# Layer 3's last sums in another order, leftover tests in front of them, and one wide product folded into a small one

## The chip, the cores and the metric

The kernel runs on one core of one Trainium2 chip. The metric is device time in microseconds, the median of a few executions. A core has TensorE (PE, matrix products into PSUM), VectorE (DVE), ScalarE (ACT), GpSimd (POOL) and SyncE (SP), each with an instruction queue of its own that it works through in order; the queues wait for one another by semaphores.

## The reference, cut to what matters

The model is four graph layers over 4096 nodes with 64 features. Each layer normalizes x, applies relu, passes the result through a layer with the 4096 x 4096 adjacency matrix of zeros and ones, and adds that to x. The change lies in the last one, layer 3, from the sums over the adjacency on:

```python
def weighted_midpoint_lincomb(A, X):
    gamma = lambda_x(X)
    num = A @ (gamma * X)
    den = A @ (gamma - 1.0)
    sgn = jnp.where(den >= 0.0, 1.0, -1.0)
    den = sgn * jnp.maximum(jnp.abs(den), DEN_EPS)
    two_mean = num / den
    mid = mobius_scalar_mul(0.5, two_mean)
    alpha = jnp.sum(A, axis=1, keepdims=True)
    return mobius_scalar_mul(alpha, mid)
...
XW = mobius_matvec(W, X)
AXW = weighted_midpoint_lincomb(A_hat, XW)
return expmap0(jax.nn.relu(logmap0(AXW)))
```

`mobius_scalar_mul`, `logmap0` and `expmap0` scale each row by a function (tanh, artanh) of its length. So per node the layer needs 64 sums of `num`, one of `den`, one of `alpha`, and then a chain of small row-wise operations.

## The kernel before, in words

The adjacency is kept on the chip as 0/1 tiles in fp8 (`A8`), made by a load that casts. That casting load is only right if the matrix holds nothing but zeros and ones, and so `checks()` loads each such tile once more in fp32 (`whole`) and has VectorE test it (1024 wide, with an accumulated count in `odd`). Every 16 tests, and at the end, the counts are summed into `odds`; at the very end PE adds `odds` over the partitions by a one-column product (`flag_ps`), VectorE casts that to `flag`, and all engines read the flag to choose between this kernel and a general one. The tests are background work.

An object `Weave` decides, while the program is built, in which order the instructions of the foreground (the sums on PE) and of the pieces of other work stand in each engine's queue. It keeps an estimated time per engine. `weave.add` puts in a generator of operations; `weave.draw()`, called between products, puts in those operations that would be ready by then; `weave.until(key, DONE)` forces pieces until a result is marked done; background pieces (`weave.back`) are left alone while `weave.quiet` is true. It is set true at the last chunk of layer 2. Once built, the order is fixed: each engine runs its queue in that order, whatever the real times.

Nodes are 32 blocks of 128 (`NB`), in four quarters of 8 blocks (`QB`, `NQ` is 4). Layer 3's features of quarter q, `S3[q, 0]` and `S3[q, 1]`, come from the end of layer 2 by `post2b` and `pre3`, one quarter after another; the key `(4, q)` is marked when quarter q is there. Each row of S3 has 196 numbers: three bf16 parts of the 65 features, and a one for `alpha`.

The outputs are eight chunks u of 512 nodes. `sum3(u, place, lo, hi)` adds blocks lo to hi into chunk u: for each of four groups of 128 nodes, one product per block, with a 128 x 128 piece of A as weights and S3 as the moving part, 196 wide. A chunk's sums lie in two one-bank PSUM tiles (place 0 and 1) or in one two-bank tile (place 2). A full chunk is 128 products, a quarter 32. `take3(u)` folds them out of PSUM: ScalarE copies the first 65 columns and alpha, VectorE adds the other two parts, and, if the chunk was summed in two goes, the part of before (`n65`, `alpha`). `summed` collects chunks: a group of three (or one chunk alone) becomes one generator `post3`, which does the row-wise chain: sign, squares of the row and of its relu, their sums `ss`, a reciprocal square root by steps (`guess`, `nt`, `ny`), artanh by Ln and by a polynomial (`po`), tanh, then x + the result, and the store. In `post3`, `r` is the tile `ny`: its first half belongs to the row's length, its second, `r[:, nb:]`, to the relu's. A predicated copy chooses between the two forms of artanh. Ln and tanh need different ScalarE tables, which `preload` brings in.

`layer3` before: chunks 0, 1, 2 sum quarters 0 and 1 and are folded as "early" parts. Then chunks 3, 4, 5 go through the quarters 0 to 3 side by side: all three quarter 0, all three quarter 1, and so on, each quarter when it is done. After that `quiet` ends and what is left of the tests is put into VectorE's queue. Then chunks 0, 1, 2 take quarters 2 and 3, and last the chunks 6 and 7 take all blocks, each as a group alone.

Of the kernel before, what the change touches and what calls it, by code (L numbers as in the profile page):

```python
# [13 lines left out]
ALU = mybir.AluOpType  # L14
# [555 lines left out]
NQ = 4  # L570
QB = 8
# [33 lines left out]
class Weave:  # L605
# [52 lines left out]
    def free(self, ps):  # L658
        k = ps.tensor.name
        self.banks[self.kind.pop(k)].append(self.used[k][0])  # L660
# [131 lines left out]
def fast_kernel(ctx: ExitStack, tc: tile.TileContext, t: dict, out: bass.AP, flag: bass.AP):  # L792
# [13 lines left out]
    NB = N // P  # L806
# [10 lines left out]
    weave = Weave()  # L817
    free = weave.free

    def one(name):  # L820
        return weave.take(1, lambda: psp.tile([P, CW], F32, tag="one", name=name, bufs=4))

    def two(name):
        return weave.take(2, lambda: psp.tile([P, 2 * CW], F32, tag="two", name=name, bufs=2))
# [4 lines left out]
    def b2(name, shape=(P, QB, D), dtype=F32):  # L829
        return b2p.tile(list(shape), dtype, tag="b2", name=name)  # L830

    def stat(name, n):
        return small.tile([P, ST], F32, tag="st", name=name)[:, :n]
# [3 lines left out]
    DV, AC, GP, SY = (Engine(weave, x.e, x.real, True) for x in (V, S_, G_, Y_))  # L837
# [79 lines left out]
    def rows(s, width=D):  # L917
        return s[:, :, None].to_broadcast([P, s.shape[1], width])
# [12 lines left out]
    def recip(v):  # L931
        r = stat("rc", v.shape[1])
        yield DV.reciprocal(r, v)
        return r
# [38 lines left out]
    def mm(o, lhsT, rhs, start=True, stop=True):  # L973
        weave.wait(names(lhsT, rhs), names(o))
        book_pe(o, lhsT, rhs, 4 if lhsT.dtype == F32 else 1)
        nc.tensor.matmul(o, lhsT, rhs, start=start, stop=stop, skip_group_check=True)  # L976
# [52 lines left out]
    DONE = set()  # L1029
# [545 lines left out]
    def lengths(s):  # L1575

        yield DV.tensor_scalar(s, s, NORM_EPS2, None, op0=ALU.max)
        r = yield from rsqrt(s)
        n = stat("norm", s.shape[1])
        yield DV.tensor_tensor(n, s, r, ALU.mult)  # L1580
        return n, r
# [5 lines left out]
    def preload(func):  # L1587

        yield AC.activation(void, tab, func)
# [80 lines left out]
    def sum3(u, place, lo, hi):  # L1670

        if u not in dst:
            v = [two("acc3")] if place > 1 else [one("acc3") for _ in range(2)]
            dst[u] = lo, [x.rearrange("p (k n) -> p k n", n=256) for x in v]
        start, v = dst[u]
        for d in range(CB):
            o = v[0][:, d, :W3] if len(v) == 1 else v[d // 2][:, d % 2, :W3]
            cols = slice((u % 2) * CW + d * P, (u % 2) * CW + (d + 1) * P)
            for b in range(lo, hi):

                mm(o, A8[u // 2][b // 2][:, b % 2, cols], S3[b // QB, b % QB // CB][:, b % CB, :],
                   start=b == start and d % 2 == 0, stop=b == hi - 1)
                if b % 4 == 3:
                    weave.draw()

    def layer3():

        half = NB // 2
        sets = (0, 1, 2), (3, 4, 5)
        early = {}  # L1690
        for k in range(2):
            for place, u in enumerate(sets[0]):
                weave.until((4, k), DONE)
                sum3(u, place, k * QB, k * QB + QB)
                if k:
                    early[u] = take3(u)
        for lo, hi in ((0, 1), (1, 2), (2, 3), (3, 4)):
            for place, u in enumerate(sets[1]):
                weave.until((4, lo), DONE)
                sum3(u, place, lo * QB, hi * QB)  # L1700
                if hi == NQ:
                    summed(u, take3(u))
        weave.quiet = False
        while weave.back and weave.back[0][1].e == "D":
            weave.issue(weave.back[0])
        for place, u in enumerate(sets[0]):
            sum3(u, place, half, NB)
            summed(u, take3(u, early.pop(u)))
        for place, u in enumerate((6, 7)):
            sum3(u, place, 0, NB)  # L1710
            summed(u, take3(u), alone=True)
        while weave.back:
            weave.force(True)
        others = nc.values_load(flag)
        weave.finish()
        return others
# [3 lines left out]
    def summed(u, parts3, alone=False):  # L1720
        group.append((u, parts3))
        if alone or len(group) == 3:
            weave.add(post3(group[:]))
            group.clear()
# [3 lines left out]
    def take3(u, more=None):  # L1728

        e = D + 1  # L1730
        n65 = b2("n65", (P, CB, e))
        alpha = stat("alpha", CB)
        at = 0
        for ps in dst.pop(u)[1]:
            k = ps.shape[1]
            o = n65[:, at:at + k, :]
            S_.activation(o, ps[:, :, :e], AF.Copy)
            S_.activation(alpha[:, at:at + k], ps[:, :, 3 * e], AF.Copy)
            V.tensor_tensor(o, o, ps[:, :, e:2 * e], ALU.add)
            V.tensor_tensor(o, o, ps[:, :, 2 * e:3 * e], ALU.add)  # L1740
            at += k
            free(ps)
        if more is not None:
            V.tensor_tensor(n65, n65, more[0], ALU.add)
            V.tensor_tensor(alpha, alpha, more[1], ALU.add)
        return n65, alpha

    def post3(parts3):

        nb = CB * len(parts3)
        sgn, den, ss = stat("sgn", nb), stat("den", nb), stat("ss", 2 * nb)
        part = [slice(i * CB, (i + 1) * CB) for i in range(len(parts3))]
        vs = [n65[:, :, :D] for u, (n65, al) in parts3]
        for h, v, (u, (n65, al)) in zip(part, vs, parts3):
            d = n65[:, :, D]
            yield DV.tensor_scalar(sgn[:, h], d, 0.0, 2.0, op0=ALU.is_ge, op1=ALU.mult)  # L1760
            yield DV.scalar_tensor_tensor(v, rows(sgn[:, h]), -1.0, v, op0=ALU.add, op1=ALU.mult)
            sq = b2("sq")
            yield AC.activation(sq[:, :CB, :], v, AF.Square)
            yield DV.scalar_tensor_tensor(sq[:, CB:, :], v, 0.0, v, op0=ALU.max, op1=ALU.mult)
            yield DV.tensor_scalar(den[:, h], d, -1.0, DEN_EPS, op0=ALU.mult, op1=ALU.max)
            yield DV.tensor_tensor(den[:, h], den[:, h], d, ALU.max)
            yield DV.tensor_reduce(ss.rearrange("p (k b) -> p k b", k=2)[:, :, h],
                                   sq.rearrange("p (k b) d -> p k b d", k=2), AX.X, ALU.add)
        yield from preload(AF.Ln)
        rd = yield from recip(den)  # L1770
        n, r = yield from lengths(ss)
        t = stat("t", nb)
        yield DV.tensor_tensor(t, n[:, :nb], rd, ALU.mult)
        ratio = stat("ratio", nb)

        def between():
            yield DV.tensor_tensor(ratio, n[:, nb:], r[:, :nb], ALU.mult)
            for h, v in zip(part, vs):
                yield DV.scalar_tensor_tensor(v, v, 0.0, rows(r[:, nb:][:, h]), op0=ALU.max, op1=ALU.mult)

        a = yield from artanh2(t, between())
        for h, (u, (n65, al)) in zip(part, parts3):
            yield DV.scalar_tensor_tensor(a[:, h], a[:, h], 0.25, al, op0=ALU.mult, op1=ALU.mult)
        yield DV.scalar_tensor_tensor(a, a, ARTANH_MAX, ratio, op0=ALU.min, op1=ALU.mult)
        yield AC.activation(a, a, AF.Tanh)
        for h, v, (u, (n65, al)) in zip(part, vs, parts3):
            yield DV.tensor_tensor(v, v, rows(a[:, h]), ALU.mult)
            x = X[u // 2][:, (u % 2) * CB:(u % 2 + 1) * CB, :]
            yield DV.tensor_tensor(x, x, v, ALU.add)
            yield SY.dma_start(out_nm[:, u * CB:(u + 1) * CB, :], x)  # L1790
# [13 lines left out]
    for step in range(2):  # L1804
        weave.add(load_gates(step))
        layer2(step, post2b if step else post2a)
    others = layer3()
    return others

# [84 lines left out]
```

## Time and profile before

| | |
|---|---|
| time, median of 3 | 811.44 us (811.31 to 813.11) |
| span of the profiled execution | 810.7 us |
| busy in the span: PE, DVE, ACT, POOL | 95%, 79%, 49%, 8% |
| PE's clock granted, mean | 0.988 |
| last op of VectorE that forms quarter 3 of S3 | starts 737.3, two of 0.84 us in all |
| ScalarE's first copies of chunk 5, chunk 7 (last bank) | 751.34, 789.64 |
| last add of VectorE | starts 805.05 |
| last store | issued 805.51 |

The trace names an operation by the engine, the line (nearly all stand in one helper's line, L781, so the tile names tell them apart), the output and inputs, and their size. `n` is `n65`, `acc` the PSUM sums, `whole` a tile under test. What matters here is not an engine's share of the whole span but which engine's queue the last operations stand in, and what the first of them waited for. Each line of the chain of waits is a start, a length and the engine and tile that the end depended on at that time.

### The profile page before, as it was taken

What the parts mean: (1) busy time and instruction counts of PE and PEld (TensorE: products, weight loads), DVE (VectorE), ACT (ScalarE), POOL (GpSimd) and SP (SyncE); (2) the same over time, 40 slices, a digit from 0 to 9 for tenths busy, and PEclk for the clock granted to TensorE, in tenths of its full rate; (3) what the DMA queues carried; (4) which work ended last, traced back from release to release, by engine and by line L of the source; (5) the groups of instructions that cost most, each with busy time, mean ns of one, the idle gap of its engine ahead of it and who ended that gap; (6) DMA issues with size and microseconds to landing.
All of it is one profiled execution on the core that took longest, in us unless ns stands there. A gap on an engine that the chain in (4) does not pass through costs nothing.

```text
span 810.7 us, 12099 instructions
## 1 busy us (share of the span) xinstructions
PE 772.4 (95%) x4473; PEld 355.6 (44%) x4494; DVE 638.3 (79%) x1433; ACT 396.9 (49%) x613; POOL 60.9 (8%) x125
## 2 busy tenths in 40 slices
PE   5999999999999999999999999999999999999990
PEld 2334444444433323333333333444444354699990
DVE  6886777677678788888888888878788787774896
ACT  5655555565565657567666664022220244462333
POOL 3333233230000000000000000000000000000000
PEclk9999999999999999999999999999999999999995
DMA  9999999998301032022022007696888910000010
GB/s 221 151 178 168 202 160 190 197 160 188 108 14 40 0 113 71 0 73 84 0 66 78 13 1 255 240 323 234 293 289 317 326 38 1 2 2 2 1 37 21
DMA packets 43954, 98.39 MB, mean 121 GB/s; under 512 B 5104, under 2 KB 20464, under 8 KB 43888
## 3 DMA queue, kind: packets, MB, share of 16 engines
q1 hardware_dynamic: 25888, 78.98, 29.0%
q0 software_dynamic: 15840, 14.42, 19.0%
q10 hardware_dynamic: 2160, 4.14, 1.4%
q8 instruction: 37, 0.61, 0.3%
q14 instruction: 29, 0.24, 0.1%
HBM read 135.54 MB, written 5.24 MB: 174 GB/s over the span
## 4 chain that ended last, share of the span: by engine, by line
PE 85%; DVE 10%; issue 1%; ACT 1%; DMA 1%; SPq 0%; ACTq 0%; DVEq 0%
PE acc L976 51%; PE score L976 14%; PE cnt L976 13%; DVE n L781 2%; PE rz L976 2%; DVE sig L781 2%; PE ps_t L980 1%; PE ps_l L976 1%; DVE ss L781 1%; DMA whole<-in_adjT 1%; DVE nt L781 1%; PE ps_kq L976 1%; PE ih L976 1%; ACT sig L781 1%; PE ps_n L980 1%
## 5 line engine op out<-in xcount | busy, mean ns | idle before, releaser
L781 ACT ACTIVATE sig<-score,fatt_add,fatt_mul 128x1024 f32<-128x1024 f32 x128 | 148.1, 1200 | 86.9 <-PE score L976 86.3
L781 DVE TENSOR_TENSOR sig<-sig,A 128x1024 f32<-128x1024 f32 x128 | 151.5, 1221 | 40.2 <-ACT sig L781 39.5
L781 DVE SCALAR_TENSOR_TENSOR whole<-whole 128x1024 f32<-128x1024 f32 x128 | 153.1, 1219 | 6.0 <-DMA whole<-in_adjT 5.6
L781 ACT ACTIVATE w<-cnt 128x512 int16<-128x512 f32 x198 | 111.2, 595 | 89.8 <-PE cnt L976 88.5
L976 PE MATMUL score<-qd,kT 64*128 64x512 f32 x512 | 129.6, 623 | 0.0
L976 PE MATMUL acc<-sig,S 128*64 128x512 f32 x512 | 125.7, 608 | 1.5 <-DVE sig L781 1.4
L976 PE MATMUL acc<-A,hm 128*128 128x512 fp8e4 x512 | 115.7, 380 | 0.0
L976 PEld LDWEIGHTS <-hm 128*128 128x128 bf16 x768 | 73.4, 98 | 90.1 <-issue 10.0
L976 PE MATMUL cnt<-A,ftri 128*128 128x512 fp8e4 x256 | 97.7, 384 | 8.2 <-ACT A L781 8.0
L976 PE MATMUL cnt<-A,fupd 128*128 128x512 fp8e4 x248 | 95.5, 385 | 2.6 <-DVE w L781 1.5
L976 PE MATMUL acc<-S,A 128*128 128x196 bf16 x1024 | 88.2, 247 | 0.0
L976 PEld LDWEIGHTS <-A 128*128 128x128 fp8e4 x1024 | 87.1, 96 | 1.1 <-issue 0.8
L976 PEld LDWEIGHTS score<-qd,kT 64*128 64x128 f32 x512 | 44.0, 187 | 81.2 <-ACT sig L781 39.2
L781 DVE TENSOR_SCALAR w<-cnt 128x512 int16<-128x512 f32 x58 | 40.1, 691 | 45.4 <-PE cnt L976 41.0
L976 PE MATMUL acc<-w,hm 128*128 128x512 bf16 x235 | 71.0, 379 | 0.9 <-issue 0.2
L860 POOL DMA_DIRECT2D A<-in_adjT x110 | 59.2, 540 | 120.0 <-DMA A<-in_adjT 119.1
L976 PEld LDWEIGHTS acc<-sig,S 128*64 128x64 f32 x512 | 30.5, 136 | 83.5 <-issue 39.9
L976 PEld LDWEIGHTS <-lo 128*64 128x64 bf16 x768 | 36.8, 109 | 58.4 <-issue 36.2
L976 PE MATMUL acc<-A,lo 128*64 128x512 fp8e4 x512 | 59.2, 381 | 0.0
L781 ACT ACTIVATE mt<-acc 64x512 f32<-64x512 f32 x32 | 18.9, 591 | 67.6 <-PE acc L976 67.1
L976 PEld LDWEIGHTS <-fupd 128*128 128x128 bf16 x248 | 24.3, 98 | 46.1 <-issue 24.3
L1655 POOL MEMSET S<- 128x4 bf16 x8 | 0.9, 116 | 546.9 <-PE ps_l L976 502.2
(185 smaller groups left out, 640.1 us busy)
## 6 DMA issues: line engine op xcount, KB each, us to landing
whole<-in_adjT SPq DMA_DIRECT2D x128, 512.0 KB, 7.1
A<-in_adjT POOLq DMA_DIRECT2D x110, 128.0 KB, 13.6
qd<-qs SPq DMA_DIRECT2D x16, 128.0 KB, 2.8
mx<-gs SPq DMA_DIRECT2D x16, 128.0 KB, 8.1
xT<-gs SPq DMA_DIRECT2D x8, 256.0 KB, 7.3
x<-in_x SPq DMA_DIRECT2D x6, 256.0 KB, 6.5
xs<-x SPq DMA_DIRECT2D x4, 256.0 KB, 4.8
qs<-qT ACTq DMA_DIRECT2D x4, 256.0 KB, 6.4
```

Of the source, the lines that this page charges most:

```text
L781: return fn(*args, **kw)
L860: nc.gpsimd.dma_start(A8[q][b // 2][:, b % 2, :], a)
L976: nc.tensor.matmul(o, lhsT, rhs, start=start, stop=stop, skip_group_check=True)
L980: nc.tensor.transpose(o, src, ident)
L1655: nc.gpsimd.memset(S3[q, c][:, :, 3 * e:], 1.0)
```

## The change

Three edits.

1. The order of the last sums. Chunks 3, 4, 5 sum quarters 0 and 1 as before. Then chunks 3 and 4 alone sum quarter 2. After the wait for quarter 3 come chunk 3's quarter 3, chunk 4's quarter 3, and chunk 5's quarters 2 and 3 together. Each chunk is folded when its sums end. The aim is that chunks 3 and 4 are ready sooner after the wait.
2. The leftover tests. The end of `quiet` and the loop that issues them stand right behind the wait for quarter 3, in front of these sums and of the folds, where they stood behind them.
3. The closing product. Before, `between` multiplied each chunk's relu by the reciprocal length (256 wide per chunk), and after tanh the chunk was multiplied by the factor `a`. Now the factor itself (4 columns per chunk) is multiplied by the reciprocal length, and the relu goes into the last wide operation.

```diff
-        for lo, hi in ((0, 1), (1, 2), (2, 3), (3, 4)):
+        for k in range(2):
             for place, u in enumerate(sets[1]):
-                weave.until((4, lo), DONE)
-                sum3(u, place, lo * QB, hi * QB)
-                if hi == NQ:
-                    summed(u, take3(u))
+                sum3(u, place, k * QB, k * QB + QB)
+        for place, u in enumerate(sets[1][:2]):
+            weave.until((4, 2), DONE)
+            sum3(u, place, half, half + QB)
+
+        weave.until((4, NQ - 1), DONE)
         weave.quiet = False
         while weave.back and weave.back[0][1].e == "D":
             weave.issue(weave.back[0])
+        for place, u in enumerate(sets[1]):
+            sum3(u, place, half + QB if place < 2 else half, NB)
+            summed(u, take3(u))
         for place, u in enumerate(sets[0]):
             sum3(u, place, half, NB)
             summed(u, take3(u, early.pop(u)))
...
         def between():
             yield DV.tensor_tensor(ratio, n[:, nb:], r[:, :nb], ALU.mult)
-            for h, v in zip(part, vs):
-                yield DV.scalar_tensor_tensor(v, v, 0.0, rows(r[:, nb:][:, h]), op0=ALU.max, op1=ALU.mult)
...
         yield AC.activation(a, a, AF.Tanh)
+        yield DV.tensor_tensor(a, a, r[:, nb:], ALU.mult)
         for h, v, (u, (n65, al)) in zip(part, vs, parts3):
-            yield DV.tensor_tensor(v, v, rows(a[:, h]), ALU.mult)
+            yield DV.scalar_tensor_tensor(v, v, 0.0, rows(a[:, h]), op0=ALU.max, op1=ALU.mult)
```

## The prediction

> **What bounds the kernel now.** I read the page's shares first, then busy time by stretch, then the chain of waits, then VectorE in order of time. The page gives PE 95% and DVE 79%, but that is a mean over stages; the change lies in the last 75 us. There the stretches say this (per engine: busy us and instructions, then granted clock, DMA share, GB/s):
>
> ```profile
> core 0: us, PE busy (x) PEld busy (x) DVE busy (x) ACT busy (x) POOL busy (x), PEclk, DMA share, GB/s
> 719.00:738.20 19.20, 19.20 (x228) 19.20 (x227) 16.39 (x79) 10.50 (x24) 0.23 (x2) 1.00 0.01 1
> 738.20:751.30 13.10, 13.10 (x157) 13.10 (x155) 2.33 (x8) 1.37 (x8) 0.00 (x0) 1.00 0.01 3
> 751.30:767.80 16.50, 16.50 (x197) 16.30 (x195) 14.87 (x60) 5.72 (x18) 0.00 (x0) 1.00 0.00 1
> ...
> 789.60:805.50 15.90, 0.01 (x1) 0.00 (x0) 13.61 (x72) 7.41 (x15) 0.00 (x0) 0.64 0.06 19
> ```
>
> PE never pauses from 719.0 to 789.6. VectorE idles from 738.2 to 751.3 (2.33 of 13.10 us busy), then is full, and for 16 us after PE has stopped it alone works. The chain of waits (start, us, what) shows where it passes from PE to VectorE:
>
> ```profile
> 743.99 7.32 PE acc L976 x86
> 751.31 0.02 issue
> 751.34 0.39 ACT n L781
> ...
> 751.82 0.44 DVE n L781
> ...
> 752.71 2.30 DVE whole L781 x4
> 755.01 0.02 issue
> 755.03 0.18 DVE odd L781
> 755.21 0.02 issue
> 755.23 0.16 DVE odds L781
> ```
>
> So up to 751.3 the end is set by PE's sums of chunk 5, after that by VectorE's queue. Its first entry is two leftover tests of adjacency tiles, which are nothing to do with chunk 5. Their data were issued at 642.5 us and such loads land in a median 7.1 us, so they could have run any time after about 650. The last lines of VectorE (start, us, form, idle before) are the closing arithmetic of chunk 7:
>
> ```profile
> 803.37 0.15 DVE L781 TENSOR_TENSOR ratio<-norm,ny 128x4 f32<-128x4 f32 x1
> 803.44 0.42 DVE L781 SCALAR_TENSOR_TENSOR n<-n,ny 128x256 f32<-128x256 f32 x1
> 803.77 0.16 DVE L781 COPY_PREDICATED rc<-flow,po 128x4 f32<-128x4 int32 x1
> ...
> 804.60 0.42 DVE L781 TENSOR_TENSOR n<-n,rc 128x256 f32<-128x256 f32 x1 [0.27 <-ACT rc L781]
> 805.05 0.43 DVE L781 TENSOR_TENSOR X<-X,n 128x256 f32<-128x256 f32 x1
> ```
>
> [...] What an op costs in a queue is its spacing, which I take from the trace: a dependent small op starts 0.20 us after the one before it, a dependent 256-wide one 0.46, an independent one after a 256-wide one 0.34, after a small one 0.07 to 0.09. [...]
>
> **The change part by part.**
>
> PE's order. The built order shows that chunk 5's third quarter (32 products) goes from in front of the wait for S3_3 to just behind chunk 4; nothing else of PE moves but the test's one-column product. From 751.34 to 789.64 (ScalarE's first reads of chunk 5's and chunk 7's last bank) PE did 448 products and that one (0.12 us): 38.18/448 = 0.0852 us each. So chunk 3's last quarter starts 32 x 0.0852 = 2.7 us sooner, at about 740.4 instead of 743.15. It needs S3_3, whose last VectorE op ends at 737.74 + 0.42 = 738.16: 2.2 us of room, no stall. Chunks 3 and 4 end 2.7 us sooner, chunk 5 does not. What do the first two win? Nothing at once: their arithmetic enters VectorE's queue only when `summed` has all three, behind chunk 5's folding.
>
> The tests. They cost 2.69 us on VectorE (752.62 to 755.31). They now stand ahead of the folds of chunk 3, from 738.16 to about 740.9, when VectorE is idle. Behind them in PE's queue stands the one-column product, 20 products into chunk 3's last quarter, so at 742.1: 1.2 us after the tests end, no stall, 0.12 us of PE ahead of chunk 5's end. Chunk 3's folds wait for that product's cast, then for sums that are ready at 742.2: nothing late waits there. Group (3,4,5) begins at 751.94 + 0.80 = 752.74 instead of 755.31: 2.57 won.
>
> The closing product. `between` loses a 256-wide product per chunk, 0.34 us of queue each. Added after tanh, in the path, is one 128x12 (or 128x4) product, 0.20. The last product takes the relu in and stays 0.42 wide. Per group of three: 1.02 off, 0.20 on. For chunk 7 the saving is smaller: without the wide product the predicated copy would start at 803.49 instead of 803.77, and tanh could start at 804.08, just after its table at 804.06, instead of 804.36; then 0.20 goes on: 0.08 won.
>
> I then walked VectorE's new order with the spacings of before, and with PE's ends as the earliest times of the folds (0.48 us from PE's end to the first fold):
> - Group (3,4,5): squares and sums 3 x 1.88 from 752.74 = 758.38; chunk 0's first fold 0.53; reciprocal to `ny` 1.94 (762.39 to 764.33) = 760.85; second fold with the early part 0.94; `norm` to the ratio of artanh 1.18 = 762.97; chunk 1's first fold 0.53; polynomial 1.29; predicated copy to the min 0.63 = 765.42; chunk 1's second fold 0.94; new product 0.20; two chunks' closing 1.60 = 768.16. Chunk 2's sums end at 751.34 + 0.12 + 192 x 0.0852 = 767.82, so its fold starts at 768.30 (0.14 waited), takes 1.39; last chunk's closing 0.80; chunk 0's sign 0.46. Its first squares start at 770.95; before 774.15. **3.20 won.**
> - Group (0,1,2): squares 4.95 = 775.90; to the polynomial 3.60 less one fold plus two folds = 780.04; polynomial 1.26; to the min 0.64 and a sign 0.07 = 782.0; tanh back at 782.30; product 0.20; closing with chunk 6's sign 2.74. Chunk 6's squares start at 785.24; before 789.36. **4.12 won.**
> - Chunk 6: `ss` at 785.86; to `at` 3.13 = 788.99; chunk 7's first fold and two small ops to 789.89. There VectorE meets chunk 7's second fold, whose sums come with PE's end: 790.02 as before. From here PE's end counts again and some of the 4.12 is lost. Fold and flag load to 790.99 (as before); polynomial, tanh, closing and chunk 7's sign 3.27; chunk 7's `ss` at 794.88, before 798.61.
> - Chunk 7: 4.68 to the end of the polynomial, then 0.20, 0.39, 0.20 to tanh, 0.24 back, 0.20 and 0.46: last add at 801.25, before 805.05. **3.80 won**; 811.44 - 3.80 = **807.6 us**.
>
> **The rivals.**
> Partial: ScalarE's queue, in which the copies of the folds stand behind Square, table loads and tanh, holds a fold at two or three places; each such miss costs a table load, 1.28 us. For it: before, chunk 6's second copy ran at 779.95, after a load, though its sums were there at 778.7. Against it: by my walk each copy is ready 0.3 us or more ahead, the last folds of chunks 2 and 7 apart. One miss: 811.44 - 3.80 + 1.28 = 808.9; with a half miss more, 809.4.
> More: VectorE reaches chunk 7 early and its chain starts at PE's end. From the fold's end 790.65, sign, product, squares and sums 1.1, then 6.87 from `ss` to the end: 798.7, 6.8 won, 804.7. Against it: chunk 6's closing stands in front in the order.
> Slower: chunk 5's third quarter was PE's filling while S3_3 was formed. If PE now waits there, 32 products (2.72 us) come late, all sums with them, and if the end is then PE's: 811.44 + 2.7 = 814.1. For it: S3_3 and the test are now waited for with 2.2 and 1.2 us of room instead of 5. Against it: everything up to S3_3 stands in the same order, so 738.2 should hold.
>
> **How the numbers follow.** The walk 0.77, the partial 0.12, more 0.04, slower 0.07. Unknown are each spacing's rounding (over 100 steps, about 0.5 us), the waits of ScalarE, and the run-to-run spread of before, 811.31 to 813.11. The range takes in the walk with 1.4 us below it, since DVE steps that I took as dependent may not be, and the partial case above: 806.2 to 809.4. Faster by over 0.3% means under 809.0: the walk, more, and a part of the partial case, 0.84; within it 0.10, slower 0.06.
>
> **What would show it.** In VectorE's order of time: the tests at 738 to 741; no idle but 0.1 us at chunk 2's fold and at chunk 7's; the group of three starting at 752.7; last add at about 801.2. In PE's: no gap at 740 to 743, end at 789.6. The waits list should show no entry of PE on VectorE. Wrong would be a PE gap there, or ScalarE's copies delaying folds by a table load.

## The result and the profile after

The changed kernel takes 809.23 us (median of 7, 807.69 to 809.48) against 811.52 us for the kernel before (median of 7 in the same comparison, 811.31 to 813.11). The ratio is 0.9962, with a 95% interval of 0.9952 to 0.9972: 3.1 us less (2.3 to 3.9), by the ratio. The forecast was 807.6 us in a range of 806.2 to 809.4, and "faster by over 0.3%".

The executions of each kernel gather around two times some 1.5 us apart. In the traces of before and after PE's granted clock is 0.50 for 3.4 us near 291 us, in code that the kernels share; e1's trace has no such fall there, and its S3 is formed 737.32 - 735.87 = 1.45 us sooner than that of before (last section). The median of before fell to the lower group (811.3) and that of after to the upper (809.2). So I compare traces by a difference that is free of this: from the start of the last op pair that forms S3 (`S<-s3v`, "S3 formed" below) to the start of VectorE's last add (`X<-X,n`). It is 805.05 - 737.32 = **67.73 us** before and 801.48 - 737.23 = **64.25 us** after, so 3.48 us won.

Busy time by stretch, after the change, for the stretch behind the forming of S3 and for the one behind PE's end (same columns as in the prediction):

```profile
738.20:751.30 13.10, 13.10 (x156) 12.90 (x155) 4.87 (x15) 1.37 (x8) 0.00 (x0) 1.00 0.01 3
...
789.60:801.50 11.90, 0.00 (x0) 0.00 (x0) 9.95 (x55) 5.98 (x13) 0.00 (x0) 0.63 0.04 12
```

PE's row is as full as before. VectorE's busy time in the first stretch went from 2.33 to 4.87 us: the tests have moved into it. From 789.6 to the start of the last add PE is done and the chain is VectorE's, 11.9 us where it was 15.4; with the last add it has 55 instructions there instead of 72. VectorE in order of time (start, us, form, idle before) shows the move:

```profile
737.98 1.22 DVE L781 SCALAR_TENSOR_TENSOR whole<-whole 128x1024 f32<-128x1024 f32 x1
...
739.13 1.22 DVE L781 SCALAR_TENSOR_TENSOR whole<-whole 128x1024 f32<-128x1024 f32 x1
...
740.59 0.16 DVE L781 TENSOR_TENSOR odds<-odds,odd 128x1 f32<-128x1 f32 x1
742.18 0.15 DVE L781 CAST flag<-flag_ps 1x1 int32<-1x1 f32 x1 [1.42 <-PE flag_ps L976]
```

The tests end at 740.75, then VectorE waits 1.42 us for the one-column product. That wait costs nothing that counts: the first fold behind it starts at 742.25, some 0.2 us after ScalarE's copies of its sums (741.72 to 742.06), and it is chunk 5's fold at 751.95, behind 4.93 us of idle time, that matters. The chain of waits after the change passes there from PE to VectorE and straight on into the group of three:

```profile
742.02 0.12 PE flag_ps L976 x2
742.14 9.30 PE acc L976 x108
...
751.46 0.39 ACT n L781
...
751.95 0.44 DVE n L781
...
752.83 0.09 DVE sgn L781
```

Where `whole` and `odds` stood (752.71 to 755.39), there is now the group's arithmetic. The list of VectorE's waits from 738 us on (what waited, for what: us in total, times, longest) has four entries:

```profile
DVE n L781 <- ACT alpha L781: 7.3, 4, 4.9
DVE flag L781 <- PE flag_ps L976: 1.4, 1, 1.4
DVE rc L781 <- ACT rc L781: 0.5, 2, 0.3
DVE flow L781 <- issue: 0.4, 1, 0.4
```

The first two lie before 751.95. After that VectorE waits three times in 49.5 us: for tanh at 782.53 (0.20) and at 800.82 (0.27), and 0.36 for the reading of the flag into the engines' registers at 791.09. The last lines are:

```profile
801.02 0.42 DVE L781 SCALAR_TENSOR_TENSOR n<-n,rc 128x256 f32<-128x256 f32 x1
801.48 0.42 DVE L781 TENSOR_TENSOR X<-X,n 128x256 f32<-128x256 f32 x1
```

### The profile page after: what moved, and what is told of

It is laid out like the page before. It is cut to its first block, busy times and chain, and to the rows that moved or that the text cites. A ratio compares the mean times of both kernels' runs of the same rounds, so it can differ in the third digit from the quotient of the medians.

```text
span 807.3 us, 12119 instructions
## 1 busy us (share of the span) xinstructions
PE 774.2 (96%) x4494; PEld 356.5 (44%) x4494; DVE 637.3 (79%) x1429; ACT 397.4 (49%) x613; POOL 60.6 (8%) x125
## 4 chain that ended last, share of the span: by engine, by line
PE 86%; DVE 9%; ACT 1%; issue 1%; DMA 1%; SPq 0%; ACTq 0%; DVEq 0%
PE acc L976 51%; PE score L976 14%; PE cnt L976 14%; PE rz L976 2%; DVE n L781 2%; DVE sig L781 2%; PE ps_t L980 2%; PE ps_l L976 1%; DVE ss L781 1%; DMA whole<-in_adjT 1%; DVE nt L781 1%; PE ps_kq L976 1%; PE ih L976 1%; ACT sig L781 1%; DVE rc L781 1%
## 5 line engine op out<-in xcount | busy, mean ns | idle before, releaser
L976 PE MATMUL acc<-w,hm 128*128 128x512 bf16 x256 | 75.8, 379 | 0.0
```

## The experiments

All in one table; "won" is against the kernel before (67.73), and the medians of before in the three comparisons were 812.69 (e1 to e4), 811.59 (e5 to e8) and 812.44 (e9 to e11).

| kernel | S3 formed | last add | difference | won | median us | ratio [95%] |
|---|---|---|---|---|---|---|
| before | 737.32 | 805.05 | 67.73 | | 811.5 | |
| after | 737.23 | 801.48 | 64.25 | 3.48 | 809.23 | 0.9962 [0.9952, 0.9972] |
| e1, edit 1 alone | 735.87 | 803.63 | 67.76 | -0.03 | 812.84 | 1.0006 [0.9998, 1.0014] |
| e2, edit 2 alone | 737.68 | 803.42 | 65.74 | 1.99 | 810.91 | 0.9974 [0.9964, 0.9983] |
| e3, edit 3 alone | 737.31 | 804.23 | 66.92 | 0.81 | 810.65 | 0.9984 [0.9977, 0.9990] |
| e4, edits 2 and 3 | 737.01 | 801.29 | 64.28 | 3.45 | 809.28 | 0.9959 [0.9946, 0.9972] |
| e5, tests twice | 736.11 | 800.36 | 64.25 | 3.48 | 809.32 | 0.9963 [0.9949, 0.9976] |
| e6, third quarters late | 737.23 | 805.52 | 68.29 | -0.56 | 811.91 | 1.0003 [0.9994, 1.0012] |
| e7, chunks 6, 7 a pair | 737.44 | 801.72 | 64.28 | 3.45 | 808.80 | 0.9956 [0.9943, 0.9970] |
| e8, fronts early | 735.90 | 797.42 | 61.52 | 6.21 | 805.18 | 0.9917 [0.9904, 0.9931] |
| e9, fronts, and a pair | 737.56 | 799.99 | 62.43 | 5.30 | 807.34 | 0.9937 [0.9922, 0.9953] |
| e10, e8 and the flag late | 737.04 | 798.19 | 61.15 | 6.58 | 807.05 | 0.9935 [0.9921, 0.9950] |
| e11, e8 without edit 1 | 737.73 | 799.61 | 61.88 | 5.85 | 806.05 | 0.9923 [0.9907, 0.9938] |

Each difference is from one trace; those of before and e1, and of after, e4, e5 and e7, agree within 0.03 us.

**Each edit alone (e1 to e4).** e1 is the kernel before with only the new order of the sums:

```diff
+        for place, u in enumerate(sets[1][:2]):
+            weave.until((4, 2), DONE)
+            sum3(u, place, half, half + QB)
+        weave.until((4, NQ - 1), DONE)
+        for place, u in enumerate(sets[1]):
+            sum3(u, place, half + QB if place < 2 else half, NB)
+            summed(u, take3(u))
```

> Edit 1 alone: the new order of the sums, the tests behind them, the old closing product. Theory (the gain is the tests' 2.57 us off VectorE's queue and the folded product; chunks 3 and 4 being ready 2.7 us sooner wins nothing, because their arithmetic enters VectorE's queue only with chunk 5): the same as before, ratio 1.000 (0.998 to 1.002), last add at 805.0 us. Rival (the earlier chunks are the gain): last add about 802.4, ratio about 0.997.

It won nothing (67.76 against 67.73). The folds of chunks 3 and 4 do come sooner, their first at 740.76 - 735.87 = 4.89 us behind the forming of S3 instead of 744.91 - 737.32 = 7.59, but `summed` lets nothing go on until chunk 5 is folded too, and that is not sooner.

e2 keeps the order of before and moves only the tests:

```diff
-        for lo, hi in ((0, 1), (1, 2), (2, 3), (3, 4)):
+        for lo in range(3):
...
+        weave.until((4, NQ - 1), DONE)
         weave.quiet = False
         while weave.back and weave.back[0][1].e == "D":
             weave.issue(weave.back[0])
+        for place, u in enumerate(sets[1]):
+            sum3(u, place, 3 * QB, NB)
+            summed(u, take3(u))
```

> Edit 2 alone: the leftover tests right behind the wait for quarter 3, the sums of chunks 3, 4, 5 side by side in all four quarters as before, the old closing product. Theory: group (3,4,5) starts 2.6 us sooner, at 752.7; the end gains 2.2 to 2.6 us: last add 802.5 to 802.9, ratio about 0.997. Rival (the gain is the order): nothing, last add 805.

It won 1.99 us, less than expected. The group of three starts 2.46 us sooner, as it should; most of the 0.47 lost after that is lost in one place, told below.

e3 has the kernel before with only edit 3 (the lines of `between` and after tanh in the change's diff).

> Edit 3 alone: the closing product folded, order and tests as before. Theory: 0.8 us less for each group of three, 0.1 for each single chunk, all on the path: last add 803.2 (802.9 to 803.6), ratio about 0.998. Rival (the wide product ran in the shadow of the Ln and the Tanh table load, so it was free): last add 804.7 or later, ratio 0.9995 or more.

It won 0.81 us, not 1.8. VectorE's lines around tanh of the first group of three show why. First the kernel before:

```profile
771.31 0.17 DVE L781 SCALAR_TENSOR_TENSOR rc<-rc,ratio 128x12 f32<-128x12 f32 x1
771.40 0.42 DVE L781 SCALAR_TENSOR_TENSOR n<-sgn,n 128x256 f32<-128x256 f32 x1
771.76 0.43 DVE L781 TENSOR_TENSOR n<-n,rc 128x256 f32<-128x256 f32 x1
```

The first of these makes tanh's argument, the third needs tanh; the way to ScalarE and back takes 0.45 us. In between VectorE forms the sign product of the next group's chunk, for which it would need 0.34 us of queue anyway. The same place in e3:

```profile
770.34 0.17 DVE L781 SCALAR_TENSOR_TENSOR rc<-rc,ratio 128x12 f32<-128x12 f32 x1
770.43 0.16 DVE L781 TENSOR_SCALAR sgn<-n 128x4 f32<-128x4 f32 x1
770.79 0.17 DVE L781 TENSOR_TENSOR rc<-rc,ny 128x12 f32<-128x12 f32 x1 [0.20 <-ACT rc L781]
```

With the wide product gone only the small sign op stands there in the built order, and the sign product comes later (771.80), at its full 0.34. The second group repeats it at 785.20. By the prediction's own terms the fold is worth 2 x (1.02 - 0.20) + 0.08 = 1.72 us; less 0.34 twice that is 1.04. The trace has won 1.10 us by the start of chunk 6's squares (788.25, before 789.36, each from its S3 formed); between there and the `ss` of chunk 7 (797.78, before 798.61) 0.28 is lost again, which was not followed up. e2 loses 0.34 in the same way: 0.45 us from its argument (767.91) to the closing op (768.36), with 0.28 of that idle.

e4 has edits 2 and 3, so it is the change without its new order.

> Edits 2 and 3 without edit 1. Theory: the same as the changed kernel, whose last add is at 801.48: 801.3 to 801.7, ratio about 0.996. If edits 2 and 3 alone win 2.4 and 1.8, their sum 4.2 is more than this, since VectorE meets PE's end at the last chunk's fold. Rival (the order of the sums is needed for it): last add 803 or later.

It gives 64.28, the changed kernel's 64.25. So edits 2 and 3 are the whole gain and edit 1 none of it. The two together win 3.45 us, though alone they win 1.99 + 0.81 = 2.80: with both, VectorE no longer waits in the first group of three, because chunk 1's second fold stands between `rc<-rc,ratio` and the closing (765.58 in the kernel after). One wait for tanh in a group stays (782.53). On top of edit 2, edit 3 is worth 65.74 - 64.28 = 1.46 us.

**Are the tests really free now? (e5)** The changed kernel, with the last two tests issued twice:

```diff
+            if n > 126:
+                yield DV.scalar_tensor_tensor(a, a, 0.0, a, op0=ALU.not_equal, op1=ALU.not_equal,
+                                              accum_out=odd[:, j:j + 1])
```

> The changed kernel with each of the two leftover tests done twice, in the same place (2.3 us more of VectorE's time ahead of the folds of chunk 3). Theory (in the new place the tests fill VectorE's idle time, which still has 8.7 us up to chunk 5's fold): no change against the changed kernel; from the last op that forms S3 to the last add 64.2 to 64.5 us (64.25 in the changed kernel). Rival (they still stand in the path, only less): 66 us or more.

64.25 again: the stretch swallows two more tests without a trace at the end. The idle time there is real room, which e8 uses.

**What would a stall of PE have cost? (e6)** The changed kernel with the third quarters of chunks 3 and 4 also behind the wait for S3's last quarter, so that PE runs out of work:

```diff
-        for place, u in enumerate(sets[1][:2]):
-            weave.until((4, 2), DONE)
-            sum3(u, place, half, half + QB)
...
-            sum3(u, place, half + QB if place < 2 else half, NB)
+            sum3(u, place, half, NB)
```

> The changed kernel, but with quarter 2 of all three chunks 3, 4 and 5 behind the wait for quarter 3, not of chunk 5 alone. PE then comes to the first product that needs S3_3 at about 735.7 and has to stand until 738.1. Theory (moving chunk 5's quarter was free because 2.2 us of room were left): PE pauses 2.0 to 2.5 us near 736, its end moves to 791.5 to 792, and the last add by as much, 66.2 to 66.8 us after the last op that forms S3 (64.25 in the changed kernel). Rival (VectorE's backlog swallows a later PE): within 0.5 us of 64.25.

PE's order of time shows the pause as expected; the last add comes later than expected, and the stretches (the last column but two is PE's granted clock) show why:

```profile
737.72 5.28 PE L976 MATMUL acc<-S,A 128*128 128x196 bf16 x40 [2.14 <-DVE S L781]
```

```profile
735.60:737.70 2.10, 0.00 (x0) 0.00 (x0) 1.94 (x8) 1.66 (x4) 0.00 (x0) 1.00 0.00 0
737.70:739.00 1.30, 1.28 (x11) 1.11 (x12) 1.30 (x2) 0.00 (x0) 0.00 (x0) 0.73 0.00 0
739.00:740.00 1.00, 1.00 (x9) 0.93 (x7) 1.00 (x3) 0.00 (x0) 0.00 (x0) 0.50 0.00 0
740.00:741.00 1.00, 1.00 (x8) 0.93 (x7) 0.69 (x4) 0.00 (x0) 0.00 (x0) 0.50 0.00 0
741.00:742.00 1.00, 1.00 (x10) 0.95 (x9) 0.00 (x0) 0.34 (x2) 0.00 (x0) 0.65 0.00 0
742.00:743.00 1.00, 1.00 (x14) 0.84 (x12) 0.00 (x0) 0.00 (x0) 0.00 (x0) 1.00 0.06 16
```

The pause was 2.14 us, but the end moved by 68.29 - 64.25 = 4.04. The 40 products behind the pause took 5.28 / 40 = 0.132 us each instead of 0.085, which is 1.87 us more: 2.14 + 1.87 = 4.01. All of it reached the end, since chunk 5's fold (755.99, after: 751.95) starts the group of three. All 12 executions of e6 paid it: by time they lie about 4 us above the changed kernel's (811.5 to 811.9 and 813.1 to 813.6, against 807.7 and 809.2 to 809.5), with a lower mean granted clock (0.988 or 0.989 and 0.987, against 0.991 and 0.989). So the room at the wait for S3 was worth having, and the prediction's rival "slower" counted only the late products: in e6 the slow ones came on top, with 1.87 us.

**Chunks 6 and 7 as a pair (e7).** With VectorE the bound, one chain of small ops for two chunks should be cheaper than two:

```diff
-            summed(u, take3(u), alone=True)
+            summed(u, take3(u), alone=u == 7)
```

> The changed kernel with chunks 6 and 7 as one group of two: one chain of small ops instead of two one after the other. Theory (after PE's end the time is VectorE's chain, and chunk 6's chain stands in front of chunk 7's): VectorE waits for chunk 7's sums, then has one chain; last add 62.3 us after the last op that forms S3 (62.0 to 62.8), so about 1.9 us off, ratio to before about 0.994. Rival (PE's end and chunk 7's own chain already set the end): 64.2 or more.

Nothing was won (64.28 against 64.25). The rival named that number, but not for the reason that VectorE's order of time shows:

```profile
790.14 0.61 DVE L781 TENSOR_TENSOR n<-n,acc 128x130 f32<-128x130 f32 x2 [4.16 <-ACT alpha L781]
791.11 0.17 DVE L781 TENSOR_SCALAR sgn<-n 128x4 f32<-128x4 f32 x1 [0.36 <-issue]
```

Now VectorE stands idle for 4.16 us until PE's end: a group's arithmetic begins only when all of its chunks are folded, so chunk 6's sign, squares and sums (1.88 us), which could have run here, came behind chunk 7's fold. What the pair saved, this gave back.

**Fronts early (e8, e9, e11).** e8 takes that condition away in the changed kernel. The front of the chain (sign, squares, their sums `ss`) becomes a generator `front3` of its own, issued for each chunk as soon as that chunk is folded; only the rest waits for the group:

```diff
-        if alone or len(group) == 3:
-            weave.add(post3(group[:]))
+        if len(group) == of:
+            for done, _ in group[:-1]:
+                weave.until(("front", done), DONE)
+            weave.add(post3(group[:], shared[0]))
...
+        else:
+            weave.add(front3(shared[0], len(group) - 1, u, parts3))
```

> The changed kernel with the front of the closing arithmetic (sign, squares, their sums) entered for each chunk as it is folded, not when its group of three is complete. Theory (edit 1 wins nothing because nothing uses chunks 3 and 4 when they are ready): their fronts, 3.76 us, go into VectorE's idle time before 751.9, group (3,4,5) is through its squares at about 754.6 instead of 758.4, chunk 6's chain is over near PE's end, and the last add comes 61.6 us after the last op that forms S3 (61.2 to 62.2), 2.65 us off, ratio to before about 0.993. Rival (PE's end sets the time now): 64.2 or more.

61.52, as expected: 6.21 us won, ratio 0.9917 [0.9904, 0.9931]. It beats both kernels. Its VectorE, while PE sums chunks 4 and 5:

```profile
743.01 0.17 DVE L781 TENSOR_SCALAR sgn<-n 128x4 f32<-128x4 f32 x1
...
746.06 0.17 DVE L781 TENSOR_SCALAR sgn<-n 128x4 f32<-128x4 f32 x1
...
750.69 0.88 DVE L781 TENSOR_TENSOR n<-n,acc 128x260 f32<-128x260 f32 x2 [2.67 <-ACT alpha L781]
```

The fronts of chunks 3 and 4 now run before chunk 5's fold, and the idle time ahead of that fold is 2.67 us instead of 4.93.

e9 is e8 with chunks 6 and 7 as a pair (`summed(u, take3(u), of=2)`).

> The kernel with the early fronts, and chunks 6 and 7 as one group of two. In the pair without early fronts chunk 6's front (1.88 us) stood behind PE's end, because a group's arithmetic began only when both were folded. Theory (that is what ate the pair's gain): here chunk 6's front runs before PE's end, and the last add comes 62.4 us after the last op that forms S3 (62.1 to 62.7), against 64.28 in the pair without it. Rival (a joint chain gains nothing whatever stands in front): 64 or more.

62.43, as expected: 1.85 us better than e7. That this is chunk 6's front, and not the earlier fronts that e9 has too, shows in the trace: VectorE waits for PE's end in both (4.82 us in e9, up to chunk 7's fold at 790.28), which swallows all that was won before. From this fold to the last add it is 799.99 - 790.28 = 9.71 us, in e7 801.72 - 790.14 = 11.58. But e9 is 0.91 worse than e8, where chunk 6's whole chain runs before PE's end.

e11 is e8 with the sums in the order of before (e2's loops).

> The kernel with the early fronts, without edit 1: chunks 3, 4 and 5 side by side through all four quarters, so that chunks 3 and 4 are folded about 2.7 us later. Theory (even when their fronts are entered at once, chunk 4's front, folded at about 749.6, still ends at about 751.5, before chunk 5's fold at 751.9): last add 61.5 us after the last op that forms S3 (61.3 to 61.8), as with edit 1. Rival (edit 1 pays once the fronts are early): 62.3 or more.

61.88, just outside what was expected: the new order is worth 0.36 us here, and nothing without the fronts (e1, e4). But the earlier chunks aren't what brings it: the group's next op after chunk 5's fold (the sign of chunk 5) starts 753.45 - 737.73 = 15.72 us behind the forming of S3, in e8 751.61 - 735.90 = 15.71, so the fronts were done in time in both. The time goes later, in two waits that e8 doesn't have, for tanh in the first group and for the copy of chunk 2's sums (0.42 in all):

```profile
762.36 0.17 DVE L781 TENSOR_TENSOR rc<-rc,ny 128x12 f32<-128x12 f32 x1 [0.20 <-ACT rc L781]
...
768.79 0.88 DVE L781 TENSOR_TENSOR n<-n,acc 128x260 f32<-128x260 f32 x2 [0.22 <-ACT alpha L781]
```

**The flag's reading (e10).** e8 with the read of the flag behind the last operation of the layer:

```diff
-        others = nc.values_load(flag)
         weave.finish()
+        others = nc.values_load(flag)
```

> The kernel with the early fronts, with the reading of the flag put behind the last chunk's arithmetic instead of between chunk 7's fold and its sign. Theory (the read costs VectorE 0.36 us of idle in the last chain): last add 61.15 us after the last op that forms S3 (61.52 with the read in front), and the end not later than before. Rival (the read then comes behind the last add and lengthens the end): span beyond the last add over 6.2 us (5.8 with the read in front).

The last add came 0.37 us sooner (61.15), but the span went on for 804.5 - 798.19 = 6.31 us behind it, where e8 has 803.2 - 797.42 = 5.78. From S3 formed to the span's end it is 67.46 against e8's 67.30: the 0.36 us moved to the end. Both theories saw half of this.

## Why the prediction was right

**PE's order: right.** No gap and no wait of PE from 719 us on; chunk 7's last copy is at 789.54 (before 789.64). That chunks 3 and 4 win nothing by ending sooner is e1 and e4.

**The tests: right.** Forecast at 738.16 to about 740.9, found at 737.98 to 740.75; the group of three forecast at 752.74, starts at 752.75. That a doubled load costs nothing (e5) shows that they are hidden with room.

**The walk: right within 0.25 us to its end.**

| step | forecast | found |
|---|---|---|
| chunk 0's first fold | 758.38 | 758.37 |
| squares of group (0,1,2) | 770.95 | 771.08 |
| chunk 6's squares | 785.24 | 785.47 |
| chunk 7's `ss` | 794.88 | 795.04 |
| last add | 801.25 | 801.48 |

The 0.23 us were lost between 758 and 785, in starts that were a few hundredths later than taken.

**The closing product: right in the walk, too large as a term.** The prediction's terms add up to 1.72 us for edit 3. Measured, it is 0.81 alone (e3) and 1.46 on top of edit 2. The difference is, for the most part, what stands in the wait for tanh: 0.34 us once on top of edit 2, twice alone. The walk had that in it, since it followed the new order (it has "tanh back at 782.30" in the second group and no wait in the first); a sum of durations does not. My expectations of e2 and e3 were such sums, and both missed.

**"From here PE's end counts again": wrong by a little.** The prediction expected 0.1 us of waiting at chunk 2's fold and at chunk 7's second fold. Neither is in the waits: by then VectorE was 0.1 to 0.2 us later than forecast and the sums were there. So VectorE's queue alone sets the end from 751.95 us on, apart from the three short waits listed above. The time hardly differs, as the two were within 0.2 us of each other.

**The rivals.** No copy was held behind a table load (1.28 us from 802.57 in the trace of before, and ScalarE's next op at 803.86) for long enough to show in VectorE's waits, so "partial" did not happen; "more" would have needed chunk 6's closing out of the way (e8 gets 2.7 us of it by another road); "slower" needed the pause that only e6 made. One sum of the partial case is off: one and a half table loads are 1.92 us, so 809.6 and not 809.4, which is also the upper end of the range; the 798.7 of "more" is the end of the last add (805.48 before), not its start. And that VectorE alone works after PE has stopped passes over ScalarE's 7.41 us in that row, of which the walk takes in tanh and its table.

**The time itself**, 809.23, is 1.6 us above 807.6 although the trace moved nearly as forecast (last add 3.57 us sooner, 3.80 forecast). The prediction took 3.80 from 811.44, the median of before; but the trace that it was worked out on is of an execution of 812.75 us, one with the half clock near 291 us. The profiled execution after has it too and took 809.22: 3.53 us less, like with like. The forecast of the gain was 0.3 us too large, and the rest is the level it was taken from. So the measured median lies only 0.2 us inside the range, by room that was put there for the partial case; that part is luck.

## What to carry to other kernels

Walk the queue of the engine that bounds the stage, in the order as built, with start-to-start spacings from the trace; a sum of the durations of what was removed missed by more than a factor of two in e3, because taking ops out also changes which op fills a wait for another engine. Background work in front of a late fold belongs into idle time before it, but see first what gathers results into groups: an earlier result is worth nothing until something may start on it (e1, and 64.25 against e8's 61.52). And take the difference from the profiled execution's own time, not from a median that mixes executions with and without a fall of the clock.

## What the runs showed of the hardware that was not expected

A pause of PE of 2.14 us cost nearly twice its length (e6): the granted clock stayed at 1.00 during it, fell to 0.50 some 0.6 us after PE had begun again, and came back after about 3.4 us (0.70 us of the stretch with mean 0.73, two full ones at 0.50, 0.70 us of the one with mean 0.65).

A shorter pause was followed by the same fall in some executions and not in others. All 13 traces have one of 1.8 us that ends near 291 us. In ten of them the clock then stands at 0.50 for 3.4 us, from some moment 0.1 to 1.8 us after PE has begun again (before: from about 292.4 us, after: from about 290.9); in e1, e5 and e8 it doesn't fall, and S3 is formed at 735.9 to 736.1 instead of 737.0 to 737.7. The mean granted clock on record for each execution splits the same way (before: 0.989 or 0.990 in those up to 811.9 us, 0.987 or 0.988 in those from there to 813.4). Before and e1 (the pause, and the stretch from 293 to 294):

```profile
290.58 0.66 PE L980 MATMUL ps_t<-fident,k 128*128 128x128 f32 x4 [1.79 <-DVE k L781]
293.00:294.00 1.00, 1.00 (x4) 0.34 (x2) 0.48 (x2) 0.40 (x1) 0.00 (x0) 0.50 0.52 78
```

```profile
290.77 0.66 PE L980 MATMUL ps_t<-fident,k 128*128 128x128 f32 x4 [1.79 <-DVE k L781]
293.00:294.00 1.00, 1.00 (x6) 0.20 (x2) 0.67 (x2) 0.71 (x1) 0.00 (x0) 1.00 0.44 61
```

Behind pauses of 0.93 and 1.14 us (ending at 269 and 677) the clock stays at 1.00 in the traces of before and after (269 to 280 and 677 to 690). So in this case a pause of 1.8 us was already followed by the half clock in ten traces of 13, and one of 1.14 us wasn't in these two. Why one execution is hit and another not, no run here shows.

A round trip from VectorE to ScalarE for a tanh of 12 columns and back costs 0.45 us, whether VectorE has something to do in it (771.31 to 771.76 before) or not (770.34 to 770.79 in e3). The reading of one flag into the engines' registers holds VectorE for 0.36 us, and moved to the end it lengthens what follows the last add from 5.78 to 6.31 us. Without any such move the changed kernel's tail is 807.3 - 801.48 = 5.82 us against 5.65 before; in e1 to e9 and e11 it is 5.67 to 5.88, so the 0.17 may be no more than the spread of single executions.
